# Scan tiles of two slots, a wider GpSimd share of B's product, and one addition moved from GpSimd to VectorE, in a linear-attention and Mamba kernel

## The chip, the cores and the metric

The kernel runs on one core of a Trainium2 chip. The metric is device time in microseconds (us): the median of 3 runs before the change is 8270.86 us (8269.19 to 8271.96). One further execution was recorded by the hardware profiler. All arithmetic is fp32 but for one small bf16 mask matmul.

## The reference

The input x has 8 samples of 512 channels and 48 x 48 = 2304 positions. Two layers are applied, each on a group-normalised x and each added to its input.

```python
x = x + linear_causal_attention(gn(x))      # 8 heads, feature elu(t)+1, numerator / denominator
x = x + mamba_cascade(gn(x))                # 4 groups of 128 channels, one after the other
# in a group: delta = softplus(dt @ Wdt), dA = exp(delta * A), dBu = delta * xs * B
h = dA * h + dBu                            # a scan over 2304 positions, 256 channels x 16 states
y = sum_n(h * C) + xs * D;  y = (y * silu(z)) @ Wo
fused = max(x_i, y);  out_i = w_local * x_i + w_global * fused   # also added to the next group's input
```

The denominators of the attention are reciprocals, one for each head and position. The two weights of the last line are sigmoids of means over all positions.

## The kernel before, in words

The positions are cut into NC = 6 columns of LC = 384. A **job** is one column of one group of one sample, so that there are 8 x 4 x 6 = 192 jobs. Two streams (even and odd samples) take turns in blocks of six jobs. A job has SLOTS = 8 **slots**, and a slot scans 128 partitions x 4 groups x 384 positions, four scans. 1536 slots in a fixed order, written out in `slot(k)`, make up the main loop. Every slot is cut into two halves. The half with number h runs `beside(h)` after all of a slot's earlier work has been issued (at the slot's start, and again after its second scan), and this places all other work. Each other piece of work is a generator that yields the half at which its next step is due, and the number of PSUM banks that this step takes. `beside` first steps those attention chunks (`heads`) whose next step takes no bank, then the tasks in their order, then the remaining chunks.

A slot k needs these pieces:

- `last_product` (L871 to L885) takes a tile `u` (tag "u", five buffers of 4 x 385 elements), copies in the old state on ScalarE (L878) and multiplies the last TAIL = 152 columns of B and dxr on GpSimd (L879). It is issued after the second scan of slot k - 2.
- `product` (L890) multiplies the other 232 columns on VectorE, from a copy of B in PSUM (`Bp`, L863). In slot 7 the product of the slot after next is issued too, behind the second scan.
- `decay` (L900, ScalarE) writes dA into a PSUM bank, `scan` (L910, VectorE) runs over `u` in place.
- `weigh` (L923, GpSimd) multiplies `u` by C, and `gather` (L937, TensorE) adds up the states into `yp`.

There are six PSUM banks for everything but `yp` and `Bp`. A decay holds one until its scan has read it.

Around the slots run four other kinds of work. The attention chunk (`chunk`, one in each job's time) forms a reciprocal `rd` (L433, L434), spreads it by a ScalarE copy to `rdb` (L441) and three TensorE transposes (L445) and multiplies q by it on VectorE (L450). Its first steps for a group 0 normalise `xn` on GpSimd, four operations (L324). The statistics of the attention's norm need a short VectorE chain for each sample (L190 to L211). A job's `prepare` forms delta, dx (L834, GpSimd, twice a job) and so on. When a slot has s = 2, the job before is closed: `gated` (L949) on VectorE, the output projection (L955) on TensorE, and `maximum` (L966) on VectorE half a slot later. At last `pass_on` mixes the finished column with TensorE (L678), copies the mix to `fu` (L682) and adds it to the attention's result in `xa` (tile xo) on GpSimd (L696), from where it is stored. That is done in 186 of the 192 jobs' columns; the last six have a path of their own on VectorE (L644).

The half of these steps counts from `first`, the first half of the job that the column feeds, which is a multiple of 16. [...]

Of the kernel before, what the change touches and what calls it, by code (L numbers as in the profile page):

```python
# [9 lines left out]
F32 = mybir.dt.float32  # L10
# [7 lines left out]
P = 128  # L18
# [1 line left out]
LC = 384  # L20
NI, NQ, NGR = 4, 4, 4
SLOTS = 8
TAIL = 152
BANKS = 6
DEPTH = 3
LEAD = 11
# [23 lines left out]
def attention_then_mamba_kernel(  # L50
# [174 lines left out]
    def statistics(b):  # L225

        xv = x[b].rearrange("(t p) l -> p t l", p=P)
        stats = small.tile([P, 4, NC, 6], F32, tag="stats_a", name=f"stats_a{b}", bufs=2)
        if b == 0:

            xs = []

            def load(c):
                t = mpool.tile([P, 4, 1 + LC], F32, tag="u", name=f"xs_{c}", bufs=5)[:, :, 0:LC]
                nc.sync.dma_start(out=t, in_=xv[:, :, c * LC : (c + 1) * LC])
                xs.append(t)

            for c in range(5):
                load(c)
            load_projections()  # L240
            for c in range(NC):
                for ct in range(4):
                    nc.vector.bn_stats(stats[:, ct, c, :], xs[c][:, ct, :])
                if c == 0:
                    load(5)
                    fetch(0)
        else:
            when = begins[b] + b % 2
            for i in range(4 * NC):
                yield (when - 4, 1) if b > 1 else "1", 0  # L250
                xs = piece(b, i)
                yield (when, 1) if b > 1 else "1", 0
                nc.vector.bn_stats(stats[:, i // NC, i % NC, :], xs)
                when += PERIOD
        norms[b] = yield from group_norm(stats, 4, f"a{b}", 2)
# [24 lines left out]
    def chunk(m):  # L280
# [156 lines left out]
        nc.scalar.copy(S[:, kept_states, :], ds[:, 0:more, :])  # L437
        bank.free()
        yield at(15), 0
        rdb = new("rdb", 1, (P, 2 * NT, 64))  # L440
        nc.scalar.copy(rdb, rd.unsqueeze(2).to_broadcast([P, 2 * NT, 64]))  # L441
        yield at(17), 1
        rb = bank()[:, 0:LC].rearrange("p (i t) -> p i t", i=NT)
        for i in range(NT):
            nc.tensor.transpose(  # L445
                rb[:, i, :], rdb[:, 2 * i : 2 * i + 2, :].rearrange("p e d -> p (e d)"), ident
            )
        yield at(18), 0

        nc.vector.tensor_mul(q, q, rb.rearrange("p i t -> p (i t)"))  # L450
# [14 lines left out]
        for i in range(NT):  # L465
            for h, sc in zip(heads_of, scs):
# [5 lines left out]
                    stop=i == NT - 1,  # L472
                    skip_group_check=True,
                )
        yield at(20), 0
        sms = []
        for par, sc in enumerate(scs):
            sm = new(f"sm{par}", 1, (P, NT, T))
# [43 lines left out]
    class Stream:  # L522
# [55 lines left out]
        def pass_on(self):  # L578
# [49 lines left out]
            if last and self.z:  # L628

                got = [  # L630
                    mpool.tile([P, 4, 1 + LC], F32, tag="u", name=f"end_{i}", bufs=5)
                    for i in range(NC // 2)
                ]
                for c in range(NC):
                    fu, xa = (got[c // 2][:, c % 2 * 2 + i, 0:LC] for i in range(2))
                    cols = slice(c * LC, (c + 1) * LC)
                    rows = slice(old[1] * P, (old[1] + 1) * P)
                    nc.sync.dma_start(out=xa, in_=x1s[old[0]][rows, cols])
                    nc.sync.dma_start(out=fu, in_=old[3][:, cols])
                for c in range(NC):  # L640
                    fu, xa = (got[c // 2][:, c % 2 * 2 + i, 0:LC] for i in range(2))
                    cols, icols = slice(c * LC, (c + 1) * LC), slice(3 + c * LC, 3 + (c + 1) * LC)
                    for t, i in ((xi[:, icols], 0), (fu, 1)):
                        nc.vector.scalar_tensor_tensor(  # L644
                            xa, t, wt[:, i : i + 1], xa, ALU.mult, ALU.add
                        )
                    nc.sync.dma_start(out=out[old[0], rows, cols], in_=xa)
                return
            if old is not None:
                mix = small.tile([P, 3, P], F32, tag=f"mix{self.z}", name=f"mix_{old[2]}", bufs=1)  # L650
                factors = [wt[:, 0:1], wt[:, 1:2]]
                if not last and not self.fresh:
                    factors.append(norm[:, 0, :])
                for i, factor in enumerate(factors):
                    nc.scalar.activation(mix[:, i, :], ident, AF.Copy, scale=factor)
            now = loads(0) if old is None or last else None
            for c in range(NC):

                cols, icols = slice(c * LC, (c + 1) * LC), slice(3 + c * LC, 3 + (c + 1) * LC)
                if now is None:  # L660
                    first = 2 * self.jobs[self.block * NC + c].start
                    yield (first - 33, 1), 0
                    now = loads(c)
                    yield (first - 25, 1), 0 if old is None else 1
                else:
                    yield "1", 0 if old is None else 1
                fu, xb, xa = now
                now = None
                if not last:
                    normed = dict(bias=norm[:, 1, :], scale=norm[:, 0, :])  # L670
                if old is None:
                    nc.scalar.activation(xi[:, icols], xb, AF.Identity, **normed)
                else:
                    bank = Banks()
                    mixed = bank()[:, 0:LC]
                    more = len(factors) == 3
                    for i, src in enumerate((xi[:, icols], fu)):
                        nc.tensor.matmul(  # L678
                            mixed, mix[:, i, :], src, start=i == 0, stop=i == 1, skip_group_check=True
                        )  # L680
                    yield "1", 0
                    nc.scalar.copy(fu, mixed)  # L682
                    if more:
                        nc.tensor.matmul(
                            mixed, mix[:, 2, :], xb, start=False, stop=True, skip_group_check=True
                        )
                    yield "1", 0
                    if more:
                        nc.scalar.activation(
                            xi[:, icols], mixed, AF.Identity, bias=norm[:, 1, :]  # L690
                        )
                    elif not last:
                        nc.scalar.activation(xi[:, icols], xb, AF.Identity, **normed)
                    bank.free()
                    self.ready = c + 1
                    nc.gpsimd.tensor_tensor(xa, xa, fu, ALU.add)  # L696
                    save(out[old[0], old[1] * P : (old[1] + 1) * P, cols], xa)
                self.ready = c + 1
                if last and c + 1 < NC:
                    yield "3", 0  # L700
                    now = loads(c + 1)

    class Job:
# [167 lines left out]

        def last_product(self, s):

            shape, cols = [P, NGR, TAIL], slice(LC - TAIL, LC)
            h, q = s // NQ, s % NQ
            u = mpool.tile([P, NGR, 1 + LC], F32, tag="u", name=f"u_{self.n}_{s}", bufs=5)
            if self.c:
                nc.scalar.copy(u[:, :, 0], self.state[:, h, q, :])  # L878
            nc.gpsimd.tensor_tensor(  # L879
                u[:, :, 1 + LC - TAIL :],  # L880
                self.B[q // 2][:, q % 2, cols].unsqueeze(1).to_broadcast(shape),
                self.dxr[h][:, :, cols],
                ALU.mult,
            )
            return u  # L885

        def product(self, s, u):

# [104 lines left out]
    class Task:  # L993
# [16 lines left out]
        def due(self):  # L1010
# [4 lines left out]
                return half_no[0] >= when  # L1015
            return half_no[0] - self.last >= int(when[0])

        def finish(self):
            while self.need is not None:
                self.step()  # L1020
# [52 lines left out]
    def beside(half):  # L1073

        half_no[0] = half
        flush(every=False)
        begin(half // 2 + LEAD)

        for t in heads:
            if t.need is not None and t.need[1] == 0 and t.fits() and t.due():  # L1080
                t.step()
        held = False
        for t in tasks + heads:
            while t.need is not None and t.due():
                if not t.fits() or held and t.need[1]:
                    held = held or t.need[1] > len(spare)
                    break
                t.step()
        prune()
# [54 lines left out]
    def prime(k):  # L1144
        job, s = at(k)
        hurry(k, lambda: job.prepared)
        primed.add(k)
        job.inputs(0)
        for r in range(2):
            us[k + r] = job.last_product(s + r)  # L1150
        job.product(s, us[k])
        ahead(DEPTH)

    def slot(k):
# [12 lines left out]
        for i in range(4):  # L1167
# [8 lines left out]
            if i == 1:  # L1176
# [11 lines left out]
                    j.inputs(0)  # L1188
                if not end and k + 2 < slots and not apart(k + 2):
                    j, r = at(k + 2)  # L1190
                    us[k + 2] = j.last_product(r)
                    if s == 7:

                        j.product(r, us[k + 2])
# [114 lines left out]
```

## Time and profile before

| what | us |
|---|---|
| median of 3 runs | 8270.86 |
| the profiled execution | 8283.94 |
| its span, first to last instruction | 8282.2 |
| first scan starts, last scan ends (timeline) | 195.1, 8258.8 |
| VectorE busy | 7829.1 |
| GpSimd busy | 7753.9 |
| TensorE busy | 7354.5 |
| ScalarE busy | 6991.8 |

Busy time is a union of spans. Two instructions that follow each other on VectorE or GpSimd overlap in the records by 0.04 to 0.09 us, so that what an instruction adds to a queue is its start-to-start time: 0.855 us for a scan recorded as 0.939, 1.017 for the product recorded as 1.100, 3.138 for a weighing recorded as 3.187, 1.44 for a last product recorded as 1.488. The profiled execution took 0.16% more than the median run.

### The profile page before, as it was taken

To read this page: it belongs to the slowest core of one execution; us is meant where nothing else is said; L and a number is where in the kernel's file an instruction comes from. 1 tells how busy PE (TensorE), PEld (TensorE's weight loads), DVE (VectorE), ACT (ScalarE), POOL (GpSimd) and SP (SyncE) were. 2 spreads that over 40 slices of the span, in tenths; PEclk is the share of its full clock that TensorE was granted. 3 is DMA by queue.
4 is the path that set the end of the run, shared out by engine and by line. 5 is a ranking of instruction groups with operands and counts; after the bars stand their busy time and mean duration, and the time that the engine had idled before them with its cause. 6 is when DMAs were issued, how large, how long until landed. Compare 5 with 4: busy or idle time off the path is not lost. (4 is left out here: it accounts for less than half of the span.)

```text
span 8282.2 us, 133009 instructions
## 1 busy us (share of the span) xinstructions
PE 7354.5 (89%) x39882; PEld 3572.9 (43%) x39882; DVE 7829.1 (95%) x10534; ACT 6991.8 (84%) x14914; POOL 7753.9 (94%) x3905
## 2 busy tenths in 40 slices
PE   8889999998889999998889999999988999998975
PEld 4444444444444444444444444444444444444421
DVE  3999999999999999999999999999999999999998
ACT  3888888888888888888888888888888888888876
POOL 2999999999999999999999999999999999999998
PEclk9999999999999999999999999999999999999976
DMA  6777778777777788777787777877777777777765
GB/s 201 189 189 206 206 200 210 205 196 205 206 200 201 199 210 209 203 205 197 204 213 201 199 206 203 210 207 197 209 204 203 203 201 195 200 200 195 191 170 146
DMA packets 1097348, 1654.99 MB, mean 200 GB/s; under 512 B 143913, under 2 KB 989353, under 8 KB 1096498
## 3 DMA queue, kind: packets, MB, share of 16 engines
q1 hardware_dynamic: 1096626, 1646.48, 76.6%
q8 instruction: 316, 5.18, 0.3%
q14 instruction: 406, 3.33, 0.1%
HBM read 1318.23 MB, written 327.68 MB: 199 GB/s over the span
## 5 line engine op out<-in xcount | busy, mean ns | idle before, releaser
L910 DVE TENSOR_TENSOR_SCAN u<-bank,u 128x385 f32<-128x385 f32 (+1 forms) x6144 | 5447.2, 939 | 115.2 <-ACT bank L900 112.9
L923 POOL TENSOR_TENSOR u<-u,C 128x1536 f32<-128x1536 f32 x1536 | 4894.5, 3187 | 349.1 <-DVE u L910 210.3
L900 ACT ACTIVATE bank<-dr,scales 128x385 f32<-128x385 f32 (+1 forms) x6144 | 3414.1, 579 | 612.8 <-DVE u L910 574.6
L879 POOL TENSOR_TENSOR u<-B,dxr 128x608 f32<-128x608 f32 x1536 | 2286.1, 1488 | 14.5 <-DMA x<-xr 13.8
L300 PE MATMUL bank<-xn,wq 128*128 128x384 f32 x4608 | 1886.5, 558 | 286.1 <-DVE u L910 233.4
L890 DVE TENSOR_TENSOR u<-Bp,dxr 128x928 f32<-128x928 f32 x1536 | 1690.2, 1100 | 10.9 <-ACT Bp L863 7.2
L937 PE MATMUL yp<-u,cst 128*32 128x384 f32 x12288 | 1353.7, 513 | 200.8 <-POOL u L923 122.8
L300 PEld LDWEIGHTS bank<-xn,wq 128*128 128x128 f32 x4608 | 955.4, 216 | 1189.5 <-DVE u L910 373.4
L722 PE MATMUL bank<-xi,wk 128*128 128x384 f32 x3072 | 1102.4, 502 | 7.6 <-ACT xr L508 7.0
L722 PEld LDWEIGHTS bank<-xi,wk 128*128 128x128 f32 x3072 | 555.9, 191 | 561.4 <-DVE u L910 107.7
L937 PEld LDWEIGHTS yp<-u,cst 128*32 128x32 f32 x12288 | 249.1, 109 | 776.7 <-issue 415.7
L900 ACT ACT_TABLE_LOAD x382 | 490.1, 1283 | 6.8
L312 ACT ACTIVATE ex<-bank,bqkv_sb 128x384 f32<-128x384 f32 x384 | 221.4, 577 | 311.5 <-PE bank L300 311.4
L863 ACT COPY Bp<-B 128x464 f32<-128x464 f32 x768 | 420.5, 548 | 21.3 <-DVE u L890 13.1
L834 POOL TENSOR_TENSOR dx<-delta,xs 128x384 f32<-128x384 f32 x384 | 386.0, 1005 | 21.5 <-ACT delta L793 21.5
L678 PE MATMUL bank<-xi,mix 128*128 128x384 f32 x372 | 175.4, 554 | 249.6 <-ACT sm L479 241.4
L955 PE MATMUL bank<-yz,scales 128*128 128x384 f32 x768 | 329.1, 541 | 51.3 <-DVE yz L949 41.7
L782 PE MATMUL bank<-dbc,steps_w 9*128 9x384 f32 x768 | 306.4, 519 | 22.3 <-DVE rd L433 17.6
L733 PE MATMUL bank<-xi,scales 128*128 128x384 f32 x768 | 296.3, 496 | 18.9 <-ACT xs L758 18.8
L769 PE MATMUL bank<-xs,scales 128*40 128x384 f32 x768 | 285.0, 494 | 0.0
L498 PE MATMUL bank<-sm,v 128*64 128x128 f32 x2304 | 254.7, 299 | 0.0
L878 ACT COPY u<-state 128x4 f32<-128x4 f32 x1280 | 249.2, 195 | 0.0
(123 smaller groups left out, 8193.6 us busy)
## 6 DMA issues: line engine op xcount, KB each, us to landing
dr<-dscr SPq DMA_DIRECT2D x1536, 192.0 KB, 4.7
dxr<-xscr SPq DMA_DIRECT2D x1536, 192.0 KB, 5.3
xn<-xn SPq DMA_DIRECT2D x192, 768.0 KB, 5.1
B<-scr SPq DMA_DIRECT2D x1536, 96.0 KB, 4.2
C<-scr SPq DMA_DIRECT2D x1536, 96.0 KB, 2.6
dscr<-delta SPq DMA_DIRECT2D x192, 384.0 KB, 4.8
xscr<-dx SPq DMA_DIRECT2D x192, 384.0 KB, 2.9
xn<-in_x SPq DMA_DIRECT2D x48, 768.0 KB, 5.1
```

The lines of the kernel that those rows point to most:

```text
L300: nc.tensor.matmul(ps, wqs[m // NC][:, kt, j * P : (j + 1) * P], xn[:, kt, :], start=(kt == 0), stop=(kt == 3),)
L722: nc.tensor.matmul(xc, wk[:, k, h * P : (h + 1) * P], xi[:, c0 + k : c0 + k + LC], start=(k == 0), stop=(k == 3),)
L782: nc.tensor.matmul(vp, steps_w[32:41, s, h * P : (h + 1) * P], dbc[32:41, :], start=True, stop=True)
L834: nc.gpsimd.tensor_tensor(dx[:, h, :], delta[:, h, :], xs[:, h, :], ALU.mult)
L863: nc.scalar.copy(self.Bp, self.B[pair % 2][:, :, 0 : LC - TAIL])
L879: nc.gpsimd.tensor_tensor(u[:, :, 1 + LC - TAIL :], self.B[q // 2][:, q % 2, cols].unsqueeze(1).to_broadcast(shape), self.dxr[h][:, :, col ...
L890: nc.vector.tensor_mul(u[:, :, 1 : 1 + LC - TAIL], self.Bp[:, s % 2, :].unsqueeze(1).to_broadcast(shape), self.dxr[s // NQ][:, :, cols],)
L900: nc.scalar.activation(dA[:, cols], self.dr[h][:, g, cols], AF.Exp, scale=w_a[:, self.w[1], NGR * h + g, q : q + 1],)
L910: nc.vector.tensor_tensor_scan(u[:, g, cols], dA[:, cols], u[:, g, cols], 0.0, ALU.mult, ALU.add,)
L923: nc.gpsimd.tensor_tensor(u[:, :, 0:LC], u[:, :, 1:], self.C[q // 2][:, q % 2, :].unsqueeze(1).to_broadcast([P, NGR, LC]), ALU.mult,)
L937: nc.tensor.matmul(self.yp[g * 32 : g * 32 + 32, 0:LC], state_sum, u[:, g, 0:LC], start=False, stop=s % NQ == NQ - 1, skip_group_check=True,)
L955: nc.tensor.matmul(self.xm[:, 0:LC], w_out[:, self.w[1], h, :], self.yz[:, h, :], start=(h == 0), stop=(h == 1),)
```

## The change

TAIL goes from 152 to 176. A tile `u` now holds two slots (three buffers in place of five), and `last_product` serves both at once: one ScalarE copy of states and one GpSimd instruction of 2 x 4 x 176 = 1408 elements, issued in the even slots only. The VectorE product shrinks from 4 x 232 to 4 x 208 elements, and the copy `Bp` from 2 x 232 to 2 x 208.

The reciprocals are no longer copied to `rdb` and transposed. TensorE multiplies each column of `rd`, broadcast over 64 columns as the stationary operand, by the identity: six small matmuls a chunk in place of three transposes. Their step, at half 17 of the chunk, is marked "first" and joins the early loop of `beside`; the step that turns the scores into `sm` on ScalarE is marked "late" and leaves it.

In `pass_on` the addition xa + fu moves from GpSimd, 23 halves ahead of the job, to VectorE, 17 halves ahead, for the 180 columns that are not the last ones; the column's loads are issued three halves later. The last six columns of stream 0 are mixed on ScalarE and GpSimd. The tile `mix` is one for both streams and is filled later. The six loads of the first statistics go out together.

```diff
-TAIL = 152
+TAIL = 176
@@ statistics, first sample
+                if c % 2 == 0:
+                    halves.append(
+                        mpool.tile([P, 2, NGR, 1 + LC], F32, tag="u", name=f"xs_{c}", bufs=3)
+                    )
+                t = halves[c // 2][:, c % 2, :, 0:LC]
...
-            for c in range(5):
+            for c in range(NC):
                 load(c)
             load_projections()
...
-                    load(5)
                     fetch(0)
@@ chunk
-        rdb = new("rdb", 1, (P, 2 * NT, 64))
-        nc.scalar.copy(rdb, rd.unsqueeze(2).to_broadcast([P, 2 * NT, 64]))
-        yield at(17), 1
+        yield at(17), 1, "first"
         rb = bank()[:, 0:LC].rearrange("p (i t) -> p i t", i=NT)
         for i in range(NT):
-            nc.tensor.transpose(
-                rb[:, i, :], rdb[:, 2 * i : 2 * i + 2, :].rearrange("p e d -> p (e d)"), ident
-            )
+            for e, h in enumerate(heads_of):
+                nc.tensor.matmul(
+                    rb[h, i, :],
+                    rd[:, 2 * i + e : 2 * i + e + 1].to_broadcast([P, 64]),
+                    ident,
+                    start=True,
+                    stop=True,
+                )
...
-        yield at(20), 0
+        yield at(20), 0, "late"
@@ pass_on
-                    yield (first - 33, 1), 0
+                    yield (first - 30, 1), 0
                     now = loads(c)
                     yield (first - 25, 1), 0 if old is None else 1
...
+                elif last:
+                    nc.scalar.activation(fu, fu, AF.Copy, scale=wt[:, 1:2])
+                    nc.scalar.activation(xi[:, icols], xi[:, icols], AF.Copy, scale=wt[:, 0:1])
+                    yield "1", 0
+                    nc.gpsimd.tensor_tensor(fu, fu, xi[:, icols], ALU.add)
+                    yield "1", 0
+                    nc.gpsimd.tensor_tensor(xa, xa, fu, ALU.add)
+                    save(out[old[0], old[1] * P : (old[1] + 1) * P, cols], xa)
...
-                    nc.gpsimd.tensor_tensor(xa, xa, fu, ALU.add)
+                    yield (first - 17, 1), 0, "late"
+                    nc.vector.tensor_add(xa, xa, fu)
                     save(out[old[0], old[1] * P : (old[1] + 1) * P, cols], xa)
@@ last_product
-            shape, cols = [P, NGR, TAIL], slice(LC - TAIL, LC)
+            shape, cols = [P, 2, NGR, TAIL], slice(LC - TAIL, LC)
             h, q = s // NQ, s % NQ
-            u = mpool.tile([P, NGR, 1 + LC], F32, tag="u", name=f"u_{self.n}_{s}", bufs=5)
+            u = mpool.tile([P, 2, NGR, 1 + LC], F32, tag="u", name=f"u_{self.n}_{s}", bufs=3)
             if self.c:
-                nc.scalar.copy(u[:, :, 0], self.state[:, h, q, :])
+                nc.scalar.copy(u[:, :, :, 0], self.state[:, h, q : q + 2, :])
             nc.gpsimd.tensor_tensor(
-                u[:, :, 1 + LC - TAIL :],
-                self.B[q // 2][:, q % 2, cols].unsqueeze(1).to_broadcast(shape),
-                self.dxr[h][:, :, cols],
+                u[:, :, :, 1 + LC - TAIL :],
+                self.B[q // 2][:, :, cols].unsqueeze(2).to_broadcast(shape),
+                self.dxr[h][:, :, cols].unsqueeze(1).to_broadcast(shape),
                 ALU.mult,
             )
-            return u
+            return u[:, 0], u[:, 1]
@@ Task, beside, slot
+        def early(self):
+            return self.need[2] == "first" if len(self.need) > 2 else self.need[1] == 0
...
-            if t.need is not None and t.need[1] == 0 and t.fits() and t.due():
+            if t.need is not None and t.early() and t.fits() and t.due():
                 t.step()
...
-                    us[k + 2] = j.last_product(r)
+                    if s % 2 == 0:
+                        us[k + 2], us[k + 3] = j.last_product(r)
```

More of the change, by code (lines that the diff above doesn't have):

```diff
@@ L229, in statistics @@
         if b == 0:
-            xs = []
+            xs, halves = [], []
             def load(c):
-                t = mpool.tile([P, 4, 1 + LC], F32, tag="u", name=f"xs_{c}", bufs=5)[:, :, 0:LC]
+                if c % 2 == 0:
[3 more added lines that the diff above has]
+                t = halves[c // 2][:, c % 2, :, 0:LC]
                 nc.sync.dma_start(out=t, in_=xv[:, :, c * LC : (c + 1) * LC])
                 xs.append(t)
-            for c in range(5):
+            for c in range(NC):
                 load(c)
@@ L630, in pass_on @@
                 got = [
-                    mpool.tile([P, 4, 1 + LC], F32, tag="u", name=f"end_{i}", bufs=5)
-                    for i in range(NC // 2)
+                    mpool.tile([P, 2, NGR, 1 + LC], F32, tag="u", name=f"end_{i}", bufs=3)
+                    for i in range(2)
                 ]
+                got = [got[0][:, 0], got[0][:, 1], got[1][:, 0]]
                 for c in range(NC):
@@ L649, in pass_on @@
             if old is not None:
-                mix = small.tile([P, 3, P], F32, tag=f"mix{self.z}", name=f"mix_{old[2]}", bufs=1)
                 factors = [wt[:, 0:1], wt[:, 1:2]]
@@ L653, in pass_on @@
                     factors.append(norm[:, 0, :])
-                for i, factor in enumerate(factors):
-                    nc.scalar.activation(mix[:, i, :], ident, AF.Copy, scale=factor)
+                mix = None
             now = loads(0) if old is None or last else None
@@ L665, in pass_on @@
                 else:
-                    yield "1", 0 if old is None else 1
+                    yield "1", 0
                 fu, xb, xa = now
@@ L672, in pass_on @@
                     nc.scalar.activation(xi[:, icols], xb, AF.Identity, **normed)
-                else:
+                elif last:
[3 more added lines that the diff above has]
+                    nc.gpsimd.tensor_tensor(fu, fu, xi[:, icols], ALU.add)
+                    yield "1", 0
+                    nc.gpsimd.tensor_tensor(xa, xa, fu, ALU.add)
+                    save(out[old[0], old[1] * P : (old[1] + 1) * P, cols], xa)
+                else:
+                    if mix is None:
+                        mix = small.tile([P, 3, P], F32, tag="mix", name=f"mix_{old[2]}", bufs=1)
+                        for i, factor in enumerate(factors):
+                            nc.scalar.activation(mix[:, i, :], ident, AF.Copy, scale=factor)
                     bank = Banks()
@@ L691, in pass_on @@
                         )
-                    elif not last:
+                    else:
                         nc.scalar.activation(xi[:, icols], xb, AF.Identity, **normed)
@@ L1148, in prime @@
         job.inputs(0)
-        for r in range(2):
-            us[k + r] = job.last_product(s + r)
+        us[k], us[k + 1] = job.last_product(s)
         job.product(s, us[k])
```

## The prediction

> **What bounds the kernel now.** The page comes first: which engine is full, and with what.
>
> ```profile
> PE 7354.5 (89%) x39882; PEld 3572.9 (43%) x39882; DVE 7829.1 (95%) x10534; ACT 6991.8 (84%) x14914; POOL 7753.9 (94%) x3905
> ...
> L910 DVE TENSOR_TENSOR_SCAN u<-bank,u 128x385 f32<-128x385 f32 (+1 forms) x6144 | 5447.2, 939 | 115.2 <-ACT bank L900 112.9
> L923 POOL TENSOR_TENSOR u<-u,C 128x1536 f32<-128x1536 f32 x1536 | 4894.5, 3187 | 349.1 <-DVE u L910 210.3
> ...
> L879 POOL TENSOR_TENSOR u<-B,dxr 128x608 f32<-128x608 f32 x1536 | 2286.1, 1488 | 14.5 <-DMA x<-xr 13.8
> ...
> L890 DVE TENSOR_TENSOR u<-Bp,dxr 128x928 f32<-128x928 f32 x1536 | 1690.2, 1100 | 10.9 <-ACT Bp L863 7.2
> ```
>
> VectorE is the bound at 95%, but GpSimd is full to 94% and waits almost only for VectorE's scans. A job lasts (8258.8 - 195.1) / 192 = 42.0 us, of which GpSimd works 40. The waits of VectorE name what it loses:
>
> ```profile
> DVE q L450 <- PE bank L445: 143.2, 129, 4.2
> DVE u L910 <- ACT bank L900: 112.9, 137, 4.8
> ```
>
> By its timeline, the first lies in half 5 of a job (slot 2), the second in half 15 (slot 7), behind ScalarE's silu batch. The start costs another 138 us; the rest is small.
>
> One more row decides: a VectorE operation on 4 elements, both inputs in SBUF.
>
> ```profile
> L198 DVE TENSOR_TENSOR gm_a<-gm_a x8: 162/3177/3632, 22.8 to 6009.6; 128x4 f32<-128x4 f32 x8
> ```
>
> Its minimum is 162 ns and its median 3177. The timelines of VectorE and of GpSimd at 1699.68 us say why:
>
> ```profile
> 1699.68 3.18 DVE L198 TENSOR_TENSOR gm_a<-gm_a 128x4 f32<-128x4 f32 x1
> 1702.89 1.39 DVE L199 TENSOR_TENSOR gm_a<-gm_a,mv_a 128x4 f32<-128x4 f32 x1
> ```
>
> ```profile
> 1699.68 3.17 POOL L923 TENSOR_TENSOR u<-u,C 128x1536 f32<-128x1536 f32 x1 [2.15 <-DVE gm_a L191]
> 1702.79 1.47 POOL L879 TENSOR_TENSOR u<-B,dxr 128x608 f32<-128x608 f32 x1
> ```
>
> Each of the two ends when GpSimd's instruction ends. None of VectorE's large operations does this: each reads one operand from PSUM, or has only one.
>
> [...]
>
> **The change, part by part.**
>
> *Product.* From 384 elements in 549 ns to 928 in 1100 is 1.01 ns an element; 96 fewer save 0.097 us, 0.78 a job, 149 in all. Two of the eight lie before the ScalarE wait of slot 7 and only lengthen it.
>
> *ScalarE.* 640 fewer state copies of 0.195, 192 rdb copies of 0.495 and 768 Bp copies shorter by some 0.04 take off 250 us. VectorE waits for ScalarE at one place, 0.56 us a job, so little of it counts: I take it in there.
>
> *Reciprocals.* TensorE now does rb ahead of the output projection (L955), but the projection's reader, L966, follows two VectorE operations later. Three transposes take 0.49 us and the twelve small matmul records of the new form some 0.94 (as those of L467 do), 0.45 more. Before, VectorE waited for projection and rb together; after, it does 0.93 us of work and then waits for the same sum plus 0.45. So a job gains the smaller of its wait and 0.48 us: 0.33 on average, not 0.75. In the 36 jobs with xn work TensorE waits for GpSimd's last xn operation, which a longer product ahead of it makes later by up to 1 us.
>
> *GpSimd's product.* What 1408 elements cost no row shows. Recorded times and elements:
>
> ```profile
> L834 POOL TENSOR_TENSOR dx<-delta,xs 128x384 f32<-128x384 f32 x384 | 386.0, 1005 | 21.5 <-ACT delta L793 21.5
> ...
> L553 POOL TENSOR_TENSOR wk<-wk,wi 128x256 f32<-128x256 f32 x20 | 14.4, 728 | 3.3 <-DMA wk<-in_wconv 3.3
> ```
>
> 256, 384 and 608 elements (728, 1005, 1488 ns) lie on one line, 175 + 2.16 N, whatever their rows: 3.22 us for 1408. From 608 to the weighing's 1536 the slope is only 1.83, which gives 2.95. These are the bounds. I take 3.15, near the first, since L879 is the same operation and lies on that line; 3.11 start to start, against 2 x 1.44 before: +0.23 a pair, +0.92 a job. The addition takes 0.96 away. GpSimd is as full as before.
>
> *The addition on VectorE.* 180 x 0.465 us (as L386) start to start, 84 us, if nothing is in its way. It reads xa and fu, both in SBUF. It comes in half 15, behind L512, when GpSimd is at this (a job without xn work, GpSimd, then VectorE):
>
> ```profile
> 2722.25 3.19 POOL L923 TENSOR_TENSOR u<-u,C 128x1536 f32<-128x1536 f32 x1
> 2725.39 1.49 POOL L879 TENSOR_TENSOR u<-B,dxr 128x608 f32<-128x608 f32 x1
> 2728.49 3.18 POOL L923 TENSOR_TENSOR u<-u,C 128x1536 f32<-128x1536 f32 x1 [1.61 <-DVE u L910]
> ```
>
> ```profile
> 2725.00 0.55 DVE L512 BATCH_NORM_STATS2 stats_m<-xr 128x6 f32<-128x384 f32 x1
> 2725.47 0.94 DVE L910 TENSOR_TENSOR_SCAN u<-bank,u 128x385 f32<-128x385 f32 x1
> 2727.39 2.65 DVE L910 TENSOR_TENSOR_SCAN u<-bank,u 128x385 f32<-128x385 f32 x3 [0.98 <-ACT bank L900]
> ```
>
> The addition would stand at 2725.47. GpSimd is idle there from 2725.4 on, if the L879 in between moves to slot 6. But there it sits ahead of slot 6's weighing, which then ends 1.67 us later or more: the addition waits for it, and behind it VectorE's last two scans, for which GpSimd's next weighing waits. The two engines are in lockstep once a job.
>
> *The loop that results.* From one slot-7 weighing to the next GpSimd has eight weighings, 25.10; four pairs, 12.44; two dx, 1.91. Then, idle: the addition, two scans and the signal, 0.47 + 1.71 + 0.21. Sum 41.84 us. VectorE's own path is shorter than before by 0.78 + 0.33 + 0.3 (the ScalarE wait) - 0.47 = 0.94. A job lasts the longer of both. Jobs before, by the timeline's first scans: the first 12, without an addition, 41.55; 143 without xn work 41.75 on average (many near 40.9, some above 42.5); 36 with it 43.32. Job by job, the 143 become 0.23 longer, +33 us. With xn work the loop has four more operations of 0.63, 44.37: +52. The first 12 save 11. Sum **+74 us**: 8284 becomes 8358 for the profiled execution; it stood 13 above the median of the runs shown, so the median becomes **8345**.
>
> *At nothing:* the first loads and weights (the start waits for statistics and chunks one after the other; four us either way), the tail (GpSimd's twelve last additions run beside the other stream's scans; uncovered, 6 us), loads three halves later (13 us before use, 5 to land), "late" (TensorE and ScalarE order only; it takes ScalarE's sm out of the way of 361 us of TensorE waits that no VectorE wait follows). SP's queue gains: the pair reads B earlier, so that loads into B wait less.
>
> **Rivals.** *GpSimd is idle when the addition comes.* Place: half 15; for it speaks the idle window of 1.61 us before every slot-7 weighing. Then VectorE is the only bound: 191 jobs x -0.94, but +20 for xn: 161 us saved, **8110**. The point where it decides: an average block of 0.9 us eats the gain. Against it: GpSimd's lag behind slot 6's scans is already 1.1 us, and the pair adds 1.67.
>
> *The pair is cheap*, 2.95 us: the loop takes 41.04, the 143 jobs gain 49 us, the xn jobs lose 29, the first save 11: **8240**. At 3.03 us all cancels to within 0.2% (some 16 us, about what a measurement of this kernel can tell from no change).
>
> *The block is worse.* GpSimd's next instruction often starts before the last one's end, and VectorE loses that race in part of the cases (L593, two elements, up to 5.3 us). In xn jobs an xn operation follows slot 6's weighing. With 3.22 us for the pair this gives **8405**.
>
> **How the numbers follow.** The lockstep with a dear pair: 0.50, own range 8290 to 8410. Idle GpSimd: 0.22. Cheap pair: 0.17. Between: 0.11. So faster 0.39, same 0.11, slower 0.50. The range runs from the idle case to the bad one.
>
> **What would show it.** The addition's row: a mean of 0.55 us says that it is free, 1.5 to 2.5 that it is blocked. L879's row with 1408 elements: 2.95 or 3.2. L890 near 1.0 us. VectorE's waits for rb small, those of L966 for L955 large, those for ScalarE in half 15 nearly gone. GpSimd busy near 7740. The forecast is wrong if additions end at once, or if GpSimd's idle time lies elsewhere than ahead of the slot-7 weighing.

## The result, and the profile after

The changed kernel takes **8576.16 us** (8574.9 to 8578.63, 4 runs) against 8271.41 us for the kernel before, measured beside it: a ratio of 1.0368, 95% interval 1.035 to 1.0386. The direction is the forecast's, the size is not: 8345 was forecast, 8410 was the upper end of its range. The profiled span grew from 8282.2 to 8576.8 us.

The page of the changed kernel, busy line and rows of groups (after the bar: busy us, mean ns of one, idle us of the engine just before them and what ended most of it):

```profile
PE 7717.7 (90%) x41586; PEld 3675.8 (43%) x41586; DVE 8071.9 (94%) x10714; ACT 6855.6 (80%) x14086; POOL 7796.8 (91%) x2963
...
L928 DVE TENSOR_TENSOR_SCAN u<-bank,u 128x385 f32<-128x385 f32 (+1 forms) x6144 | 5422.6, 934 | 28.5 <-ACT bank L918 26.3
L941 POOL TENSOR_TENSOR u<-u,C 128x1536 f32<-128x1536 f32 x1536 | 4870.2, 3181 | 499.2 <-DVE u L928 382.1
...
L897 POOL TENSOR_TENSOR u<-B,dxr 128x1408 f32<-128x1408 f32 x768 | 2445.2, 3184 | 112.3 <-DMA B<-scr 65.3
...
L908 DVE TENSOR_TENSOR u<-Bp,dxr 128x832 f32<-128x832 f32 x1536 | 1532.5, 998 | 63.6 <-DMA dxr<-xscr 39.1
...
L714 DVE TENSOR_TENSOR xo<-xo,fu 128x384 f32<-128x384 f32 x180 | 396.8, 2204 | 0.0
```

VectorE is busy for 243 us more. The addition (L714) brings 397, the shorter product (L908, 1690.2 before) takes 158 off, and the rest nearly cancels. VectorE's idle time grows by 52. GpSimd's busy time changes by half a per cent, but its waits grow: ahead of weighings (L941) from 349 to 499 us, ahead of the pair (L897) from 14.5 to 112.3.

The rows of waits (us in total, times, longest):

```profile
POOL u L941 <- DVE u L928: 382.1, 195, 3.8
...
DVE q L456 <- PE bank L447: 145.6, 97, 6.3
...
DVE fg L984 <- PE bank L973: 90.6, 146, 2.2
...
POOL u L897 <- DMA B<-scr: 65.3, 53, 13.3
...
DVE u L928 <- ACT bank L918: 26.3, 22, 6.2
```

VectorE's wait for ScalarE (L928, 112.9 before) is mostly gone. Its wait for rb, the spread reciprocals (L456, 143.2 before), is where it was, and a wait for the output projection (L984) has come in beside it. The new row is GpSimd's pair waiting for loads into B.

Timelines of VectorE and of GpSimd at the end of a job without xn work:

```profile
2811.23 0.55 DVE L518 BATCH_NORM_STATS2 stats_m<-xr 128x6 f32<-128x384 f32 x1
2811.70 2.90 DVE L714 TENSOR_TENSOR xo<-xo,fu 128x384 f32<-128x384 f32 x1
2814.52 3.49 DVE L928 TENSOR_TENSOR_SCAN u<-bank,u 128x385 f32<-128x385 f32 x4
```

```profile
2807.85 3.18 POOL L897 TENSOR_TENSOR u<-B,dxr 128x1408 f32<-128x1408 f32 x1 [1.39 <-DMA x<-xr]
2810.99 3.20 POOL L941 TENSOR_TENSOR u<-u,C 128x1536 f32<-128x1536 f32 x1
2816.40 3.17 POOL L941 TENSOR_TENSOR u<-u,C 128x1536 f32<-128x1536 f32 x1 [2.21 <-DVE u L928]
```

The addition stands at 2811.70 and ends 0.41 us after slot 6's weighing ends (2814.19). Then come the scans, and GpSimd idles 2.21 us for them: the lockstep of the prediction. What it did not have is the 1.39 us in the first GpSimd line, the pair waiting for data, which pushes all of this back. (The bracket names the transfer that ended last by the profile.)

By first scans in the timeline, the jobs changed as follows (mean us):

| jobs | before | after | x number |
|---|---|---|---|
| first 12 | 41.55 | 42.04 | +6 |
| 143 without xn work | 41.75 | 43.20 | +207 |
| 36 with xn work | 43.32 | 45.42 | +76 |

With a start longer by 5 us this is the whole difference of 294.

### The profile page after: what moved, and what is told of

Same layout as the page of the kernel before. It is cut to its first block, busy times and chain, and to the rows that moved or that the text cites. A ratio compares the mean times of both kernels' runs of the same rounds, so it can differ in the third digit from the quotient of the medians.

```text
span 8576.8 us, 132611 instructions
## 1 busy us (share of the span) xinstructions
PE 7717.7 (90%) x41586; PEld 3675.8 (43%) x41586; DVE 8071.9 (94%) x10714; ACT 6855.6 (80%) x14086; POOL 7796.8 (91%) x2963
## 5 line engine op out<-in xcount | busy, mean ns | idle before, releaser
L928 DVE TENSOR_TENSOR_SCAN u<-bank,u 128x385 f32<-128x385 f32 (+1 forms) x6144 | 5422.6, 934 | 28.5 <-ACT bank L918 26.3
L941 POOL TENSOR_TENSOR u<-u,C 128x1536 f32<-128x1536 f32 x1536 | 4870.2, 3181 | 499.2 <-DVE u L928 382.1
L897 POOL TENSOR_TENSOR u<-B,dxr 128x1408 f32<-128x1408 f32 x768 | 2445.2, 3184 | 112.3 <-DMA B<-scr 65.3
L303 PE MATMUL bank<-xn,wq 128*128 128x384 f32 x4608 | 1976.7, 579 | 248.4 <-DVE u L928 163.3
L908 DVE TENSOR_TENSOR u<-Bp,dxr 128x832 f32<-128x832 f32 x1536 | 1532.5, 998 | 63.6 <-DMA dxr<-xscr 39.1
L955 PE MATMUL yp<-u,cst 128*32 128x384 f32 x12288 | 1411.9, 533 | 185.5 <-POOL u L941 155.4
L303 PEld LDWEIGHTS bank<-xn,wq 128*128 128x128 f32 x4608 | 993.0, 225 | 1234.7 <-DVE u L928 334.4
L800 PE MATMUL bank<-dbc,steps_w 9*128 9x384 f32 x768 | 372.7, 607 | 147.1 <-DVE u L928 133.2
L881 ACT COPY Bp<-B 128x416 f32<-128x416 f32 x768 | 389.2, 507 | 53.1 <-DMA B<-scr 36.7
L714 DVE TENSOR_TENSOR xo<-xo,fu 128x384 f32<-128x384 f32 x180 | 396.8, 2204 | 0.0
L800 PEld LDWEIGHTS bank<-dbc,steps_w 9*128 9x128 f32 x768 | 140.2, 213 | 372.2 <-ACT bank L918 242.0
```

The lines of the kernel that those rows point to most:

```text
L303: nc.tensor.matmul(ps, wqs[m // NC][:, kt, j * P : (j + 1) * P], xn[:, kt, :], start=(kt == 0), stop=(kt == 3),)
L714: nc.vector.tensor_add(xa, xa, fu)
L800: nc.tensor.matmul(vp, steps_w[32:41, s, h * P : (h + 1) * P], dbc[32:41, :], start=True, stop=True)
L881: nc.scalar.copy(self.Bp, self.B[pair % 2][:, :, 0 : LC - TAIL])
L897: nc.gpsimd.tensor_tensor(u[:, :, :, 1 + LC - TAIL :], self.B[q // 2][:, :, cols].unsqueeze(2).to_broadcast(shape), self.dxr[h][:, :, cols ...
L908: nc.vector.tensor_mul(u[:, :, 1 : 1 + LC - TAIL], self.Bp[:, s % 2, :].unsqueeze(1).to_broadcast(shape), self.dxr[s // NQ][:, :, cols],)
```

## The experiments

Each kernel ran beside the kernel before, and its median stands here with the ratio to that and the 95% interval. The medians of the kernel before lay between 8270 and 8283 us from one set of runs to another, so that a difference in us between kernels of different sets is good to some 10 us; the ratios are free of this.

### The addition alone, on either side

Back to GpSimd, in the changed kernel:

```diff
-                    yield (first - 17, 1), 0, "late"
-                    nc.vector.tensor_add(xa, xa, fu)
+                    nc.gpsimd.tensor_tensor(xa, xa, fu, ALU.add)
```

> The changed kernel with one thing undone: the addition xa + fu is back on GpSimd, right after the column's xi, as before the change. Blocked-addition theory (two SBUF inputs wait for GpSimd's instruction, 2.2 us each, and that is nearly all of the loss): most of the 305 us comes back, 8250 to 8310, although GpSimd gets 180 x 0.96 us more. Reciprocal theory (the new order on TensorE costs VectorE 0.5 us a job in slot 2, and the addition only part): the jobs look like the first 12 of the changed kernel, which have no addition and last 42.04 us: 192 x 42.04 + 224 = 8296, and still slower than before. Dear-pair theory (GpSimd's loop is what is long): no gain, 8550 or more, since GpSimd has more to do.

Measured: 8331.67 us, 1.0061 (1.0044 to 1.0078). So the move costs 244 us in the company of the other edits. That is most of the loss, though the time stays above the 8250 to 8310 that the theory of the blocked addition gave.

The move alone, in the kernel before:

```diff
-                    yield (first - 33, 1), 0
+                    yield (first - 30, 1), 0
...
-                    nc.gpsimd.tensor_tensor(xa, xa, fu, ALU.add)
+                    if not last:
+                        yield (first - 17, 1), 0
+                        nc.vector.tensor_add(xa, xa, fu)
+                    else:
+                        nc.gpsimd.tensor_tensor(xa, xa, fu, ALU.add)
```

> The kernel before, with the addition alone moved to VectorE at 17 halves ahead (loads at 30). Blocked-addition theory: GpSimd runs a last product of 1.44 us and then is idle at that place, so that the block is shorter than in the changed kernel, where the pair has pushed slot 6's weighing there: a row of 1.0 to 1.8 us, time 8270 to 8400. If the block is as long as in the changed kernel (2.2 us): 8450 or more.

Measured: 8368.93 us, 1.0116 (1.0099 to 1.0133), 97 us. Its row among the groups of instructions, and VectorE's wait for ScalarE:

```profile
L698 DVE TENSOR_TENSOR xo<-xo,fu 128x384 f32<-128x384 f32 x180 | 207.3, 1152 | 0.0
```

```profile
DVE u L914 <- ACT bank L904: 16.0, 15, 3.8
```

Alone, the addition takes 1.15 us, against 2.20 in the changed kernel: the block exists without the pair. With the pair and the reciprocals in the old form (a kernel shown below) it takes 1.89:

```profile
L711 DVE TENSOR_TENSOR xo<-xo,fu 128x384 f32<-128x384 f32 x180 | 340.3, 1891 | 0.0
```

So most of the difference comes with the pair, which puts slot 6's weighing in the addition's way, and the rest with the new reciprocals and their order. The second line above shows that VectorE's wait for ScalarE, 113 us before, goes even though ScalarE does as much as before; in the changed kernel with the addition back on GpSimd it is 133. The likely reason is that VectorE arrives later, because of the addition.

### The block taken away, the addition left on VectorE

The addition takes zeros from spare PSUM columns of `yp` in place of `fu`, so that only one operand lies in SBUF. The output then lacks the mixed column.

```diff
-                    nc.vector.tensor_add(xa, xa, fu)
+                    nc.vector.tensor_add(
+                        xa.rearrange("p (i t) -> p i t", t=P),
+                        xa.rearrange("p (i t) -> p i t", t=P),
+                        yp[:, LC : LC + P].unsqueeze(1).to_broadcast([P, 3, P]),
+                    )
...
+    nc.vector.memset(yp[:, LC : LC + P], 0.0)
```

> The changed kernel, but the addition on VectorE adds zeros from PSUM in place of fu (same elements, same place, one SBUF input; the mixed column is so left out of the output). Blocked-addition theory: its row falls from 2204 to some 550 ns and the time to 8270 to 8330. If the addition is long for another reason (it waits for loads, or it is the place in the order), the row stays near 2200 ns and the time at 8560 to 8590.

Measured: 8343.16 us, 1.0077 (1.0062 to 1.0092). The addition by tile, here and in the changed kernel (ns minimum/median/maximum, first and last start):

```profile
L714 DVE TENSOR_TENSOR xo<-xo,yp x180: 534/554/556, 656.3 to 8243.2; 128x384 f32<-128x384 f32 x180
```

```profile
L714 DVE TENSOR_TENSOR xo<-xo,fu x180: 759/2290/6212, 658.7 to 8474.5; 128x384 f32<-128x384 f32 x180
```

With one SBUF operand not a single one of 180 takes over 556 ns. The same operation in the same place is 233 us cheaper by this alone, although it now waits for TensorE's writes to `yp`, 36 us in all. It is only 11 us slower than with the addition on GpSimd (8331.67, from the same set of runs): the cost of the move is the block and hardly the work.

### The reciprocals, on either side

The new form, with "first" and "late", alone in the kernel before (the edit is that part of the diff shown above). The half-clock theory named here takes TensorE's half clock, 934 us in the trace before, for the cause of VectorE's wait in slot 2:

> The kernel before, with the reciprocals' new form and order alone. Recorded prediction: a job gains 0.33 us, so 8200 to 8230. Half-clock theory [...]: the wait moves from q to fg and the sum stays near 140 us; 8240 to 8280.

Measured: 8205.76 us, 0.9919 (0.9904 to 0.9934), a gain of 66.

```profile
DVE q L453 <- PE bank L444: 55.8, 46, 6.3
DVE fg L969 <- PE bank L958: 52.9, 126, 2.2
```

VectorE's wait for rb falls from 143 to 56, a wait of 53 for the projection (2 before) replaces part of it. Together that is 37 us less. The rest of the 66 lies elsewhere, in VectorE's wait for a ScalarE copy (L386, 31 to 16), its wait for `yp` (18 to 8) and its busy time (10 less). Jobs without xn work became 0.61 us shorter, those with it 0.18 longer. The old form put back into the changed kernel:

> The changed kernel with the reciprocals as before (ScalarE copy, three transposes, steps without first and late; the copy lies in pr's tile for want of room). Blocked-addition theory: VectorE only waits longer at the addition, since GpSimd's loop sets the job: 8540 to 8580. Reciprocal theory: the waits of q and fg fall from 236 to some 140 us and the time by about as much, 8450 to 8490.

Measured: 8598.14 us, 1.0386 (1.0371 to 1.0402). There the new form is worth 22 us by the medians, 15 by the ratios, and the intervals overlap: this isn't told from no gain. The time is above what either theory gave.

### The pair alone

The changed kernel with the addition on GpSimd and the reciprocals in the old form, that is, two-slot tiles, TAIL = 176 and the small edits of the change (the later loads, `mix`, the last six columns):

> Both undone: what is left is the two-slot tiles with TAIL 176 (and loads three halves later). If the pair itself is harmless, VectorE's products are 158 us shorter and the time is 8120 to 8180, faster than before by 1 to 2%. Dear-pair theory: GpSimd has 40.5 us of work a job plus what it must wait for, 8270 or more.

Measured: 8415.85 us, 1.0164 (1.0149 to 1.0179). VectorE has 109 us less to do (7720.3 busy), and the kernel is 133 us slower than before.

Two-slot tiles with TAIL left at 152 and the loads due as before the change:

> The kernel before, with two-slot tiles alone and TAIL still 152 (one product of 1216 elements for two slots; the reciprocal's copy lies in pr's tile, one tile mix, and the last six columns as in the changed kernel). If the pair's place in GpSimd's order is what hurts (even slots' weighings 1.4 us later), 8300 to 8400 although GpSimd does no more work than before. If its length is what hurts, 2.80 us a pair is less than two of 1.44, and the time is 8260 to 8290.

Measured: 8357.45 us, 1.0106 (1.0091 to 1.0121).

```profile
L893 POOL TENSOR_TENSOR u<-B,dxr 128x1216 f32<-128x1216 f32 x768 | 2133.4, 2778 | 33.3 <-DMA B<-scr 27.7
```

GpSimd's products cost 2133 us in place of 2286, VectorE's are as before, and still 86 us are lost. So a pair costs something apart from its length. It hardly waits for a free tile: 27.7 of the 33.3 us of idle time ahead of it are loads into B. That leaves its place in GpSimd's order as the likely cause, but the edits to `mix` and to the last six columns are in this kernel too and were not run alone. Of 36 jobs with xn work each became 1.4 us longer (44.71), the others 0.13.

Its length was then added: behind each pair of this kernel an idle GpSimd multiplication of 108 elements, whose result nothing reads.

```diff
+            idle = small.tile([P, 108], F32, tag="idle", name=f"idle_{self.n}_{s}", bufs=1)
+            nc.gpsimd.tensor_tensor(idle, cst[:, 0:108], cst[:, 108:216], ALU.mult)
             return u[:, 0], u[:, 1]
```

> The two-slot tiles with TAIL 152, and behind each pair one more GpSimd multiplication of 108 elements that nobody reads (0.41 us by the line 175 + 2.16 N): GpSimd has as much to do as with TAIL 176, VectorE as much as before. If GpSimd's length is what took the gain of the shorter products, this is well above the pair of 152 alone (1.0106 of before): 1.025 to 1.035, that is the pair of 176 (1.0164) plus what the shorter products give. If GpSimd has room for it, it stays at 1.008 to 1.014, and the loss from 152 to 176 came otherwise.

Measured: 8429.13 us, 1.0192 (1.0177 to 1.0207): 72 us for the length. That is less than was expected if the length took the whole gain, and more than if GpSimd had room for it. From here to the kernel with TAIL = 176, VectorE's products get shorter by some 150 us in all (and the later loads come in). The time falls by 0.0028, some 23 us, with intervals that just overlap.

### Is it the xn operation behind the pair?

In the kernel with the pair alone, the xn operations of a chunk are due two halves earlier:

```diff
-            yield at(-4), 0
+            yield at(-6), 0
...
-                    yield at(ct - 4), 0
+                    yield at(ct - 6), 0
```

> The kernel with two-slot tiles and 176 columns alone, in which the xn operations of an attention chunk are asked for two halves earlier. If the pair's loss comes from the last xn operation standing behind the pair, with TensorE's chunk projection and VectorE's product with rb waiting after it, the waits of VectorE for rb in the 36 jobs with xn work fall from 4 us to some 1.5, and 60 to 100 us come off: 1.005 to 1.009. If the loss comes from the loop or from GpSimd's length, it stays at 1.015 to 1.018.

Measured: 8378.91 us, 1.012 (1.0105 to 1.0135). The waits of VectorE for rb, first without and then with this edit:

```profile
DVE q L453 <- PE bank L448: 247.3, 135, 5.3
```

```profile
DVE q L453 <- PE bank L448: 129.3, 117, 5.9
```

The wait falls by 118 us (in jobs with xn work from 4.0 to 0.7 us on average), as the theory said, but the time by only 37 us, which lies between what the two theories gave. Part of the rest went into other waits and blocks of VectorE: the wait for ScalarE's decay (152.9 to 170.6), that for loads of dxr (24.2 to 43.9), and a small operation with two SBUF operands, L198, among others (again without and then with the edit):

```profile
L198 DVE TENSOR_TENSOR gm_a<-gm_a 128x4 f32<-128x4 f32 x8 | 11.0, 1379 | 0.3
```

```profile
L198 DVE TENSOR_TENSOR gm_a<-gm_a 128x4 f32<-128x4 f32 x8 | 21.0, 2626 | 0.3
```

Jobs with xn work became 1.17 us shorter. The others stayed at 42.2, where they lasted 41.75 in the kernel before. So the xn operation behind the pair is shown as a cause for less than a third of the pair's loss, and most of what is left lies in the jobs without xn work.

### The loads that the pair waits for

In the changed kernel, B's rows one half earlier, ahead of dr:

```diff
-            steps(0)
-            yield first - 7, 0
             rows(0, 0)
+            yield first - 7, 0
+            steps(0)
```

> The changed kernel with B's rows fetched one half earlier, ahead of the job's other first loads. In its profile the pair of slot 6 waits 0.64 us a job for loads into B, and in a job without xn work that wait lies in the closed loop of GpSimd and VectorE. If that loop sets the time, the wait comes off each of 180 jobs: 60 to 115 us less than the changed kernel, 8460 to 8520, ratio 1.023 to 1.030. If VectorE's own waits set the time (for rb and for the blocked addition), the loads change nothing: 8560 to 8590, ratio 1.035 to 1.038.

Measured: 8561.28 us, 1.034 (1.0325 to 1.0356). The waits of the pair then:

```profile
POOL u L897 <- DMA dxr<-xscr: 42.1, 37, 12.7
POOL u L897 <- DMA B<-scr: 29.5, 26, 2.2
```

The time lay near the range of the theory in which the loads change nothing. But the wait had only moved, from B to dxr, so that this run doesn't decide between the two. A job without xn work was shorter by 0.10 us, about as much as its wait for the pair's loads (0.64 to 0.53). SP's own rows of waits showed what was late: the store of dx, behind which B and dxr are queued, waits for GpSimd's dx. Before the change, after it, and in the kernel with the pair alone:

```profile
SPq L802 <- POOL dx L834: 1095.7, 192, 8.5
```

```profile
SPq L820 <- POOL dx L852: 1295.7, 192, 10.0
```

```profile
SPq L816 <- POOL dx L848: 1307.2, 192, 9.9
```

A late dx alone doesn't make the pair wait. With the pair alone the store is as late, and so it is in the changed kernel with the addition back on GpSimd (1339 us), but in these two the pair waits only 0.06 and 0.07 us a job for its loads. There GpSimd still has the addition to do between the second dx and the pair. From the end of dx until GpSimd is ready for slot 6's pair (or, before the change, for the last product in its place) there are 14.7 us before, 13.9 and 13.8 in these two, and 12.8 in the changed kernel. So the wait comes of the two edits together. To take it away, B went ahead of that store, and dxr directly behind it:

```diff
+            rows(0, 0)
             xsrc = spread("xscr", dx)
             spreading.clear()
             yield first - 8, 0
             flush()
-            steps(0)
+            scaled(0)
             yield first - 7, 0
-            rows(0, 0)
+            steps(0)
             yield first - 6, 0
-            scaled(0)
```

> The changed kernel with both loads of the slot 6 pair earlier: B's rows ahead of the store of dx, dxr directly behind that store, and dr after it. With B alone one half earlier the pair's wait in a job without xn work only fell from 0.64 to 0.53 us, since it then waited for dxr, and such a job became shorter by the same 0.11 us. If the closed loop sets the time and this order brings the wait to 0.15 us or less, some 0.5 us come off each of the 135 to 180 jobs without xn work: 8480 to 8510, ratio 1.025 to 1.029. If VectorE's other waits take the place of it: 8550 to 8575, ratio 1.034 to 1.037.

Measured: 8469.83 us, 1.023 (1.0213 to 1.0247), 106 us less than the changed kernel and somewhat more than was expected.

```profile
L897 POOL TENSOR_TENSOR u<-B,dxr 128x1408 f32<-128x1408 f32 x768 | 2446.8, 3186 | 13.1 <-DMA dr<-dscr 11.0
...
L908 DVE TENSOR_TENSOR u<-Bp,dxr 128x832 f32<-128x832 f32 x1536 | 1530.6, 997 | 7.8 <-DMA dxr<-xscr 7.7
...
L714 DVE TENSOR_TENSOR xo<-xo,fu 128x384 f32<-128x384 f32 x180 | 347.3, 1929 | 0.0
```

The wait ahead of the pair falls from 112.3 to 13.1, VectorE's own wait for the same dxr from 39.1 to 7.7, and the addition's row by 50 us. A job without xn work goes from 43.20 to 42.51, by about as much as the pair waited (0.64 us), as it must if the loop sets the time. Which of the two engines' waits for these loads did it is not separated, since both went.

### TensorE's clock, a side question

The trace's clock records have TensorE at half clock for 934 us before and 1542 after. Before, 117 of the 156 stretches begin 3 to 6 us ahead of a slot 2; after, 98 of 220 do, and the others lie more widely around that. Before, TensorE is busy for 58% (median) of the 3.41 us ahead of a half stretch, and for 100% (median) of the stretches of 3.41 us at full clock that are followed by another. To see whether this is a cause, six matmuls of 128 columns that nothing reads went ahead of each chunk's first projection:

```diff
+        for _ in range(6):
+            nc.tensor.matmul(yp[:, LC : LC + P], ident, ident, start=True, stop=True)
         qp, qb = project(0)
```

In the kernel before:

> The kernel before, with six matmuls of 128 columns that nobody reads ahead of each chunk's first projection, where TensorE stands idle for a bank (slot 1). Half-clock theory: the clock falls to half less often there (now 154 stretches, 934 us in all, mostly begun 4 to 5 us before slot 2), the mean clock rises from 0.944 to 0.96 or more, q's wait falls from 143 to under 90 us and the time to 8170 to 8220. If the clock has no part in it, TensorE has 1 us a job more to do ahead of q, the wait grows and the time is 8290 to 8400.

Measured: 8225.07 us, 0.9944 (0.9929 to 0.9959); half clock 508 us, mean clock 0.944 to 0.969.

```profile
DVE q L452 <- PE bank L447: 76.5, 65, 7.1
```

In the kernel with the pair alone:

> The pair with TAIL 176 alone (1.0164 of before), with the six unread matmuls ahead of each chunk's first projection. Half-clock theory: its loss is in large part TensorE at half clock (1194 us of it against 934 before), so that filling the idle stretch brings more than the 0.56% it brought before: 0.998 to 1.006. Late-GpSimd theory (TensorE's queue stands behind gathers and xn operations that GpSimd has not finished): no more than before, 1.009 to 1.014.

Measured: 8370.57 us, 1.0118 (1.0101 to 1.0135), a gain of 0.46% against 0.56% without the pair. In the kernel before, half of the wait for rb (143.2) goes when TensorE is at full clock for more of the time. But the pair's loss is no smaller with the matmuls (1.74%) than without (1.64%): it is not a matter of the clock.

### A version that beats both

Reciprocals in the new form and unread matmuls, on the kernel before:

> A version to beat both: the kernel before with the new reciprocals (0.9919) and the six unread matmuls (0.9944). Half-clock theory: both act on the same wait of 143 us in slot 2, so less than their sum: 0.987 to 0.990, 8165 to 8190. If they are independent 0.9863; if the matmuls only stand in rb's way now that it goes first, 0.992 or more.

Measured: 8167.38 us, 0.9876 (0.9861 to 0.989). With TAIL = 160 besides:

> The same with TAIL 160 and single tiles: VectorE's products 32 elements shorter (33 ns, 51 us in all), GpSimd's 32 longer (69 ns, 106 us in all). If GpSimd still has room at 94%, 0.6% below the one without; by the late-GpSimd theory nothing is gained or 0.2 to 0.6% lost.

Measured: 8170.37 us, 0.9878 (0.9863 to 0.9893), no difference. With the xn operations two halves earlier in place of that:

> The best version so far (reciprocals in the new form, six unread matmuls ahead of each chunk's projections, single tiles) with the xn operations two halves earlier. Its waits for rb in jobs with xn work are near 1 us already. If the xn operation is what these wait for, 10 to 30 us come off: 0.984 to 0.987. If not, 0.987 to 0.989.

Measured: 8160.99 us, 0.9857 (0.984 to 0.9873). Its interval and that of the first overlap, and the wait for rb hardly moved (44.6 to 42.9): not told apart. No gain from earlier xn operations is shown where no pair stands ahead of them.

## Why the prediction was right in direction and wrong in size

**Product.** Right as work: 158 us fewer on its row against 149. Wrong as a gain: with GpSimd's product as long as it is, it moved the time by only some 23 us. VectorE's own path was not the longer one.

**Reciprocals.** Right in number: 0.33 us a job, 63 in all, against 66 measured alone. That it fits so well is in part luck: the two waits that the working was about fell by only 37 us, and waits that it didn't have gave most of the rest. In the changed kernel, where VectorE waits elsewhere, the gain is too small to be told from none.

**ScalarE.** The list counted 250 us of work. The rows of copies fell by as much (state 119, rdb 95, `Bp` 31), but busy time only by 136: it is a union, in which the short copies largely overlap with their neighbours. Of a state copy's 0.195 us recorded before, 0.04 lies outside its neighbours, of an rdb copy's 0.495, 0.35. That the wait for ScalarE goes is right, but the addition does it, as the kernel with the addition alone shows.

**GpSimd's product.** Right: 3184 ns recorded against bounds of 2.95 and 3.22, 3.14 start to start against 3.11.

**The block.** Right in place, cause and size: a mean of 2.20 us where 1.5 to 2.5 was named as its sign, and 0.55 with one SBUF operand. The rival of an idle GpSimd fell with that. With both operands in SBUF, each of the 180 additions ends 0.41 to 0.45 us after a GpSimd instruction does; with zeros from PSUM they take 534 to 556 ns. VectorE's large operations in the main loop, with a PSUM operand or only one, show no block in either kernel: the product takes at most 1126 ns, a scan 961, one of 384 elements 561. But the number of operands isn't the whole cause. A small operation with one SBUF operand and a constant (wt + 1.0, two elements) takes 170 to 5287 ns before (L593) and 169 to 2572 after (L599). What the parts do together can't be had by adding them up: 97 (addition) - 66 (reciprocals) + 133 (pair) make 164, the changed kernel lost 305. The longer block behind the pair and the wait for the pair's loads are two such joint effects.

**The loop, the step that failed.** The closed loop was the right model, but its sum was too short. For a job without xn work, between the weighings of slot 7 by the timeline:

| term, us a job | forecast | measured |
|---|---|---|
| eight weighings | 25.10 | 25.16 |
| four pairs | 12.44 | 12.55 |
| two dx | 1.91 | 1.92 |
| idle for addition, two scans, signal | 2.39 | 2.45 |
| wait of slot 6's pair for loads | 0 | 0.64 |
| waits of the other weighings | 0 | 0.25 |
| small operations and their waits | 0 | 0.22 |
| sum | 41.84 | 43.19 |

Half of the miss is one line: the loads, put under "at nothing", with the remark that "SP's queue gains". The step looked at the half in which B is read and not at what stands ahead of its load in SP's queue: the store of dx. In the kernels with the pair of 1408 elements dx ends 1.3 to 1.5 us later in a job than before, and the addition's leaving GpSimd brings the pair of slot 6 nearer to dx by some 1 us, which the prediction only counted as work taken away. The kernel with earlier loads shows this term, together with VectorE's wait for the same dxr, to be worth 106 us. The two terms below it are small things that the loop of before had too (0.57 us of weighings' waits), and that a sum over large instructions leaves out. By jobs, those without xn work account for 174 us of the miss of 220 in the profiled execution, those with it for 24, the first twelve for 17, the start for 5.

**Jobs with xn work.** Forecast +52 us, measured +76. The xn wait was put at up to 1 us. In the kernel with the pair alone these jobs wait 4.0 us for rb against 1.5 before, in the changed kernel 2.4, and there another part has gone over to the projection.

**The sign to look for.** "Waits for rb small" was wrong (145.6), those for the projection large (90.6) and those for ScalarE in half 15 nearly gone (11) were right. GpSimd busy was 7797, where 7740 was named.

What stays open: how the 100 us that the pair still costs with earlier xn operations divide. Some 70 of them lie in the jobs without xn work. One part is the pair's length: of 72 us for 0.42 us behind each pair the shorter VectorE products give back about a third. What the place alone costs in these jobs was not taken apart further.

## What to carry to other kernels

Where two engines are both nearly full, write down their closed loop with every wait and every small operation in it, then trace each input of the loop back through its DMA queue to the instruction ahead of which it can't be issued: half of this miss (0.64 of 1.35 us a job) was a load behind a store behind a late product. Taking an instruction out of a queue also brings the next one nearer to the data it needs, here by some 1 us. When work goes from GpSimd to VectorE, look at where its operands lie: the addition took 2.20 us on average with both in SBUF and 0.55 with one in PSUM, and that choice alone was worth 233 us. Merging two instructions into one saved some of their time here (2778 ns for two slots, against 2 x 1488) but moves the second half of the work ahead of something: check what was queued between the two.

## What the runs showed of the hardware that was not expected

- GpSimd's two-input row follows one line from 256 to 1408 elements to about 1%: 2778 ns at 1216 and 3184 at 1408, where 175 + 2.16 N gives 2802 and 3216. The weighing, in place with 1536 elements, takes 3181, as much as 1408 elements do: it isn't on this line, which would give 3493.
- TensorE's clock records know two values, 1.0 and 0.5, and the half stretches last 3.41 us or a multiple, but for the last one (94.8 us before, 101.2 after). Not expected was that a kernel with TensorE busy to 89% still spends 934 us at half clock, and that matmuls which nothing reads gain 0.56%.
- A block of VectorE can outlast more than one GpSimd instruction. Of the longest addition, 6.21 us, the timelines of VectorE and of GpSimd show:

```profile
8333.88 6.21 DVE L714 TENSOR_TENSOR xo<-xo,fu 128x384 f32<-128x384 f32 x1
```

```profile
8332.45 3.15 POOL L897 TENSOR_TENSOR u<-B,dxr 128x1408 f32<-128x1408 f32 x1
8335.57 3.16 POOL L941 TENSOR_TENSOR u<-u,C 128x1536 f32<-128x1536 f32 x1
8338.69 0.99 POOL L682 TENSOR_TENSOR fu<-fu,xi 128x384 f32<-128x384 f32 x1
```

It lasts through the ends of two instructions, each of which is followed at once by the next, and ends 0.41 us after the third, just as the one shown above did after its one. The other 179 end so after the first GpSimd instruction to end within them, although in 36 of these the next had followed at once. So a block can go on past the end of an instruction, but in this trace it did so once in 180.
